# A graph network on one core: a fixed order of issue, an index search on VectorE in place of code matmuls, and a product moved from GpSimd to VectorE

## The chip, the core and the metric

The kernel runs on one core of a Trainium2 chip. A core has five engines that take their instructions in order, each from its own queue: TensorE (PE in the profile, its weight loads PEld), VectorE (DVE), ScalarE (ACT), GpSimd (POOL) and SyncE (SP, which here only issues DMAs). TensorE reads SBUF and writes PSUM[...]. The metric is the device time of one execution in microseconds (us); a profiled execution also gives its span, from its first to its last instruction.

## What is computed

Thirty-two graphs ("batches") of 512 nodes with 128 features and a 512 x 512 adjacency of zeros and ones, with about 3% ones, go through four residual layers. Each starts with `h = max(layernorm(x), 0)`:

```
layer 0: pre = h@(W1-W2) [node i] + h@W2 [node j] + b;  x += max over j of relu(pre) * adj[i,j]
layer 1: four times: tanh([A_rows @ (f@ws+bs), f@wn+bn, A_cols @ (f@wd+bd)] @ wu + bu), with skips
layer 2: x += (adj @ (h@weight)) / rowsum + bias
layer 3: four GRU steps: m = adj^T @ (h@w);  r, z = sigmoid(...);  n = tanh(xn + r*hn)
         h = (1-z)*n + z*h
```

The change touches how layer 0 finds the neighbours of a node, the last line of layer 3, and the order in which everything is issued.

## The kernel before

**Planning.** The Python code runs twice over the work. `prepare`, `gathers`, `layer1` and `layer23` (in `fast`, L858) note each operation in a `Flow` object (L303) with its inputs, outputs and an estimated cost. `Flow.run` (L569) then emits the instructions: of the operations that could start earliest by the estimates, on any engine, it takes the earliest, and among equals that with the earliest due time. A due time is the batch's place in steps of `PACE` less the length of the chain behind the operation (`close`, L436) less a `LEADS` entry for the stage (L41 to L68). Up to `AHEAD` = 6 parts are noted at a time, so several batches are in flight. All of this happens when the program is built; on the chip each engine has one fixed queue. Almost every instruction carries the line of the one emitting call (L529), so the profile's groups are told apart by tile names. Where the planner expects TensorE to idle for over 1 us it adds dummy matmuls (`spin`, L553).

**Layer 0.** The maximum over neighbours is taken in two ways. Columns are cut into eight half-blocks of 64. The first four neighbours within a half-block are picked by one-hot matmuls: `pc` (L1051) counts, `cc` copies the count, 16 DMAs on SP spread it into `ccd`, VectorE or ScalarE makes the one-hot `oh`, TensorE multiplies it with `qhl` into `pa`, and VectorE folds `pa` into `acc`. Neighbours beyond the fourth (up to seven for each node) are fetched as rows from a table in DRAM. For each of four column tiles `it`, TensorE writes keys into `pkey` (L1091, L1092): a matmul with `ltk` gives 1024 times the rank of a neighbour within its half-block, and a matmul with the diagonal `code` adds the row number in the table. VectorE's `max` takes the eight largest keys, and three small operations (`row`, `bad`, `idx`) decode them. The table `qtab` has 1024 rows in an interleaved order (`CODES`), written by four DMAs for each batch (L1041); the rows over 256 are filled with zeros at the start. GpSimd issues 28 indirect DMAs for each batch (`gm`, `G`, L1123), and VectorE folds the results into `gm`.

**Layers 1 to 3.** Wide products use a value split in two (`hi` made by ScalarE, `lo` by VectorE or GpSimd) times the adjacency (`pg`); weight products run on float32 data, which the trace shows as two matmul records each (`pu`, `pk`, `phn`, `pxn`). In a GRU step GpSimd makes `zc = 1-z` (L1305) and `z*h` (L1331, the group `gate<-h,gate`), and VectorE makes the rest; `h` is transposed (`ph`) and split for the next step.

**Setup.** Weights are prepared by `FastWeights` (`first`, `rest`, `last`), with the DMAs dealt in turn to SP and ACT. Batch 0's adjacency, 1 MB, is one DMA on ACT's queue.

Of the kernel before, what the change touches and what calls it, by code (L numbers as in the profile page):

```python
# [17 lines left out]
I32 = mybir.dt.int32  # L18
AF = mybir.ActivationFunctionType
# [11 lines left out]
ROWS = 1024  # L31
KEY = float(ROWS)
CODES = ((0, 1), (P, 1), (2 * P, 2), (4 * P, 4))
ONACT = (2, 2, 1, 0)
NLEFT = 7
PACE = 46.14
SPACING = 1.5
AHEAD = 6
BANKS = (1, 2, 2, 1)

LEADS = {  # L41
    "prepare": -28.3, "counts": -7.5, "keys": 16.5, "rows": 26.6,
    "gather0": 59.4, "gather1": 70.0, "gather2": 28.0, "gather3": 53.5,
    "first": 61.2, "layer1": 43.0, "layer10": 30.3, "layer11": 8.7,
    "layer12": 56.0, "layer13": -41.3, "layer2": 39.7, "layer3": 5.5,
    "layer30": 99.5, "layer31": 189.8, "layer32": 213.5, "layer33": 84.7,
    "out": 56.0,
}

LEADS0 = {  # L50
    "prepare": 18.5, "counts": 53.1, "keys": 4.8, "rows": -15.7,
    "gather0": 52.2, "gather1": 93.4, "gather2": -34.5, "gather3": -69.1,
    "first": 0.5, "layer1": 141.7, "layer10": 10.1, "layer11": 110.3,
    "layer12": -73.8, "layer13": -13.4, "layer2": 6.9, "layer3": 56.5,
    "layer30": 35.3, "layer31": 29.8, "layer32": 117.9, "layer33": 64.0,
    "out": 75.9,
}
LEADSN = {
    "prepare": -19.9, "counts": -18.3, "keys": -42.0, "rows": 46.6,
    "gather0": 15.9, "gather1": -47.7, "gather2": -77.8, "gather3": -4.3,  # L60
    "first": 13.3, "layer1": -33.7, "layer10": 14.0, "layer11": -36.5,
    "layer12": 103.7, "layer13": 62.6, "layer2": 212.2, "layer3": 99.8,
    "layer30": 182.6, "layer31": 105.8, "layer32": 85.0, "layer33": 161.6,
    "out": -15.2,
}
FIRST = (1.57, 0.36, -0.05, 0.0)
LAST = (0.0, 0.18, 0.33, 0.24, 0.3)
WEIGHTS = (-3.98, -2.44, -5.94)  # L68
# [194 lines left out]
class Op:  # L263
    def __init__(self, engine, fn, args, kw, cost, after):
        self.engine, self.fn, self.args, self.kw = engine, fn, args, kw
        self.cost, self.after = cost, after
        self.before, self.next, self.new, self.bufs = [], [], [], []
        self.waits, self.ready, self.due, self.end = 0, 0.0, 0.0, 0.0
        self.issued, self.lane, self.port, self.turn = False, None, False, 0

        self.source = engine if after < 1.0 else id(self)
# [31 lines left out]
class Flow:  # L303
# [11 lines left out]
    EVENT = 0.13  # L315
    ENGINES = ("pe", "vec", "act", "pool", "sync")

    def __init__(self, nc, pace, ahead, slack=0.0):
        self.nc, self.pace, self.ahead, self.slack = nc, pace, ahead, slack
        self.rings, self.part, self.lanes = {}, [], {}  # L320
        self.lead = 0.0
        self.free = dict.fromkeys(self.ENGINES, 0.0)
        self.busy = dict.fromkeys(self.ENGINES, 0.0)
        self.spin, self.window, self.active, self.rate = None, 0, 0.0, 1.0
        self.gathered, self.port, self.turn, self.queue = 0.0, 0.0, 0, {}
        self.seen = {e: {} for e in self.ENGINES}
        self.waiting = {e: [] for e in self.ENGINES}
        self.vec = Engine(self, "vec", nc.vector)
        self.act = Engine(self, "act", nc.scalar)
        self.pool = Engine(self, "pool", nc.gpsimd)  # L330
        self.sync = Engine(self, "sync", nc.sync)
# [22 lines left out]
    def cost(self, engine, op, outs, ins):  # L354
# [9 lines left out]
        if engine == "vec":  # L364
# [4 lines left out]
            else:  # L369
                t = (o if op != "max" else n) / 960.0 + 0.15  # L370
# [11 lines left out]
    def note(self, engine, fn, args, kw, outs, ins, cost, after):  # L382
        op = Op(engine, fn, args, kw, cost, after)
        op.lead = self.lead
# [21 lines left out]

    def spaced(self, lane, gap):

        self.part[-1].lane = (lane, gap)
# [26 lines left out]
    def close(self, n):  # L436

        part, self.part = self.part, []
        inside = {id(op) for op in part}
        lanes = {}  # L440
        for op in part:
            for u in op.before:
                u.next.append(op)
        for op in reversed(part):
            tail = max((u.due for u in op.next if id(u) in inside), default=0.0)
            op.due = tail + op.cost + op.after + self.LAT
            if op.lane:
                lane, gap = op.lane
                op.due = lanes[lane] = max(op.due, lanes.get(lane, 0.0) + gap)
        for op in part:  # L450
            op.due = n * self.pace - op.due - op.lead
            op.waits = sum(not u.issued for u in op.before)
            if not op.waits:
                self.enter(op)
        return part

    def enter(self, op):
        op.ready = max((u.end + u.after + self.lat(u, op) for u in op.before), default=0.0)
        self.waiting[op.engine].append(op)
# [6 lines left out]
    def start(self, op):  # L466
        t = max(op.ready, self.free[op.engine])
        if op.lane:
            t = max(t, self.lanes.get(op.lane[0], -op.lane[1]) + op.lane[1])
# [7 lines left out]
        if op.port:  # L477
            t = max(t, self.port)
        return t

    def step(self):
        best = None
        for e in self.ENGINES:
            now = [(t, op) for op in self.waiting[e] if (t := self.start(op)) is not None]
            if not now:
                continue
            first = min(t for t, _ in now)
            if best is None or first < best[0]:
                t, op = min(
                    ((t, op) for t, op in now if t <= first + self.slack), key=lambda c: c[1].due  # L490
                )
                best = (first, t, op)
        assert best, "nothing can be issued"
        _, t, op = best
        self.waiting[op.engine].remove(op)
# [16 lines left out]
        if op.port:  # L512
            self.port = op.end
        self.busy[op.engine] += cost
        if op.lane:
            self.lanes[op.lane[0]] = t
# [17 lines left out]
        for u in op.next:  # L534
            u.waits -= 1
            if not u.waits:
                self.enter(u)
        self.log(op, t)
# [30 lines left out]
    def run(self, parts):  # L569

        left = []
        of = {}
        oldest = 0
        while True:
            while len(left) < len(parts) and len(left) < oldest + self.ahead:
                n = len(left)
                place, make = parts[n]
                make()
                ops = self.close(place)
                left.append(len(ops))  # L580
                of.update((id(op), (op, n)) for op in ops)
            if oldest == len(parts):
                return
            op = self.step()
            _, n = of.pop(id(op))
            left[n] -= 1
            while oldest < len(left) and left[oldest] == 0:
                oldest += 1
# [34 lines left out]
class FastWeights:  # L623
# [5 lines left out]
    def __init__(self, nc, F, a, const, mid, ps):  # L629
# [28 lines left out]
        self.ltk = fixed([P, P], BF16, "ltk")  # L658
        nc.vector.tensor_scalar(self.ltk, self.lt.bitcast(F32), KEY, None, ALU.mult)
        self.code = fixed([P, n // P, P], BF16, "code")  # L660
        icode, code = fixed([P, n // P], I32, "icode"), fixed([P, n // P], F32, "fcode")
        for t, (first, step) in enumerate(CODES):
            nc.gpsimd.iota(
                icode[:, t : t + 1], pattern=[[1, 1]], base=first, channel_multiplier=step
            )
        nc.vector.tensor_copy(code, icode)
        for t in range(n // P):
            nc.vector.tensor_scalar(
                self.code[:, t, :], ident, code[:, t : t + 1], None, ALU.mult
# [57 lines left out]
    def rest(self):  # L727

        F, a, ident, NL3 = self.F, self.a, self.ident, self.NL3

# [11 lines left out]
        for key, src, m in rows:  # L742
            col[key] = at
            (F.sync, F.act)[len(col) % 2].dma_start(out=brow[at : at + m, :], in_=src)
# [22 lines left out]
        for i in range(NL1):  # L767
# [4 lines left out]
            for k, nm in enumerate(("ws", "wn", "wd")):  # L772
                w = self.temp(("f", "hg", "hT1")[k], f"{nm}{i}")[:, 0:ch, :]
                (F.sync, F.act)[k % 2].dma_start(
# [32 lines left out]
    def last(self):  # L807
# [16 lines left out]
        for l in range(NL3):  # L824
            for nm, dst in (("hh", self.gh), ("ih", self.gm)):
                q = nm == "ih"
                g = self.temp(("gate1", "xn1")[q], f"graw_{nm}{l}")[:, 0:3, :]
                (F.sync, F.act)[q].dma_start(
# [30 lines left out]
def fast(ctx: ExitStack, tc: tile.TileContext, a: dict, out: bass.AP, bad):  # L859
# [11 lines left out]
    F = Flow(nc, PACE, AHEAD)  # L871
    F.share(ps, 8, {f"ps{s}": n for s, n in enumerate(BANKS)} | {"idle": 0})

    def lead(b, stage):
        own = LEADS0 if b == 0 else LEADSN if b == B - 1 else {}
        return LEADS[stage] + own[stage] if stage in own else LEADS[stage]
# [13 lines left out]
    zero = const.tile([P, P], F32, name="zero")  # L890
    nc.gpsimd.memset(zero, 0.0)
    tables, scals = [], []
    for i in range(2):
        t = dram.tile([ROWS, P], F32, name=f"qtab{i}")
        k = (ROWS - 2 * P) // P
        nc.sync.dma_start(
            out=t[2 * P :, :].rearrange("(k p) d -> p k d", p=P),
            in_=zero.unsqueeze(1).to_broadcast([P, k, P]),
        )
        tables.append(F.fixed(t, [ROWS, P], F32))  # L900
# [3 lines left out]
    def load(b):  # L904
# [3 lines left out]
        F.act.dma_start(out=af, in_=adj[b].rearrange("(t p) j -> p t j", p=P))  # L908
# [71 lines left out]
    def prepare(b, xt, af):  # L980
# [60 lines left out]
        for t, (first, step) in enumerate(CODES):  # L1041
            F.sync.dma_start(
                out=tab[first : first + (P - 1) * step + 1 : step, :], in_=qn[:, t, :]
            )
        F.lead = lead(b, "counts")
# [796 lines left out]
```

## Time and profile before

| What | us |
|---|---|
| median of 3 runs (2909.56 to 2911.77) | 2909.67 |
| span of the profiled execution | 2909.0 |
| TensorE busy | 2795.8 |
| VectorE busy | 2299.1 |
| GpSimd busy | 1848.5 |
| ScalarE busy | 1268.4 |

The profiled span lies 0.67 us under the median of the runs, so the two can be read as one number. A stretch of the profile is read by the windows view, which gives each engine's busy time in it. Matmul records overlap their neighbours, since a matmul starts before the one ahead of it has drained; how close TensorE is to packed is therefore read from the distances between starts, not from busy time.

### The profile page before, as it was taken

What the parts mean: (1) busy time and instruction counts of PE and PEld (TensorE: products, weight loads), DVE (VectorE), ACT (ScalarE), POOL (GpSimd) and SP (SyncE); (2) the same over time, 40 slices, a digit from 0 to 9 for tenths busy, and PEclk for the clock granted to TensorE, in tenths of its full rate; (3) what the DMA queues carried; (4) which work ended last, traced back from release to release, by engine and by line L of the source; (5) the groups of instructions that cost most, each with busy time, mean ns of one, the idle gap of its engine ahead of it and who ended that gap; (6) DMA issues with size and microseconds to landing.
All of it is one profiled execution on the core that took longest, in us unless ns stands there. A gap on an engine that the chain in (4) does not pass through costs nothing.

```text
span 2909.0 us, 38588 instructions
## 1 busy us (share of the span) xinstructions
PE 2795.8 (96%) x11766; PEld 1794.6 (62%) x11766; DVE 2299.1 (79%) x5371; ACT 1268.4 (44%) x2622; POOL 1848.5 (64%) x2020
## 2 busy tenths in 40 slices
PE   7799999999999999999999999999999999999998
PEld 4565566666666665666665666666666666566675
DVE  6778888788888888888788888888888888887634
ACT  6643344444444443444443444444444444443333
POOL 3666656666666766666766666776666666666522
PEclk9999999999999999999999999999999999999999
DMA  6644334323444433334423344433344433333200
GB/s 150 136 74 88 62 85 81 83 55 76 79 86 81 83 60 78 74 83 80 87 56 78 74 84 87 82 69 64 74 84 87 81 81 56 70 66 63 55 5 9
DMA packets 191270, 218.49 MB, mean 75 GB/s; under 512 B 30376, under 2 KB 139600, under 8 KB 191056
## 3 DMA queue, kind: packets, MB, share of 16 engines
q0 software_dynamic: 47104, 92.34, 23.1%
q1 hardware_dynamic: 73768, 63.63, 7.1%
q10 hardware_dynamic: 70184, 59.98, 6.8%
q8 instruction: 96, 1.57, 0.2%
q14 instruction: 118, 0.97, 0.1%
HBM read 164.32 MB, written 17.96 MB: 63 GB/s over the span
## 4 chain that ended last, share of the span: by engine, by line
PE 85%; DVE 7%; DMA 2%; issue 2%; ACT 2%; POOL 1%; SPq 0%; ACTq 0%; DVEq 0%; POOLq 0%
PE pg L529 26%; PE pu L529 19%; PE pk L529 14%; PE pa L529 7%; PE phn L529 4%; PE pxn L529 4%; DVE acc L529 3%; PE ph L529 2%; PE pq L529 2%; PE pkey L529 2%; PE pt L529 1%; DVE lo L529 1%; PE pf L529 1%; PE po L529 1%; PE px L529 1%
## 5 line engine op out<-in xcount | busy, mean ns | idle before, releaser
L529 POOL DMA_INDIRECT G<-qtab,idx x768 | 841.3, 1095 | 653.6 <-DVE gm L529 495.3
L529 DVE TENSOR_TENSOR acc<-acc,pa 128x512 f32<-128x512 f32 x992 | 673.4, 679 | 123.3 <-PE pa L529 97.6
L529 PE MATMUL pg<-an,lo 128*128 128x512 f32 (+1 forms) x1072 | 461.9, 433 | 0.0
L529 PE MATMUL pg<-an,hi 128*128 128x512 f32 (+1 forms) x1072 | 456.1, 428 | 4.8 <-PE spin L553 1.1
L529 PE MATMUL pa<-oh,qhl 128*128 128x512 f32 x1024 | 450.5, 508 | 6.1 <-DVE acc L529 2.1
L529 PE MATMUL pu<-ag,w 128*128 128x512 f32 (+1 forms) x952 | 448.0, 568 | 4.1 <-DVE ag L529 4.1
L529 DVE TENSOR_SCALAR oh<-ccd 128x1024 fp32r<-128x1024 bf16 x492 | 348.9, 723 | 62.4 <-PE pa L529 55.0
L529 ACT ACTIVATE xn<-x,shift,rstd 128x128 f32<-128x128 f32 x512 | 214.6, 483 | 261.4 <-POOL shift L529 255.7
L529 PE MATMUL pg<-at,lo 128*128 128x512 f32 (+1 forms) x672 | 295.9, 442 | 22.8 <-DVE lo L529 22.3
L529 PE MATMUL pg<-at,hi 128*128 128x512 f32 (+1 forms) x672 | 272.7, 407 | 8.4 <-ACT hi L529 7.2
L529 PEld LDWEIGHTS pa<-oh,qhl 128*128 128x128 f32 x1024 | 191.8, 193 | 135.5 <-issue 65.9
L529 PEld LDWEIGHTS pg<-an,hi 128*128 128x128 f32 x1072 | 202.6, 189 | 107.2 <-issue 62.5
L529 PEld LDWEIGHTS pg<-an,lo 128*128 128x128 f32 x1072 | 202.7, 189 | 85.9 <-issue 52.0
L529 PE MATMUL pk<-h,g_hh 128*128 128x512 f32 (+1 forms) x528 | 246.7, 582 | 1.2 <-DVE ag L529 1.1
L529 DVE TENSOR_TENSOR gm<-gm,G 128x128 f32<-128x128 f32 x768 | 242.4, 322 | 3.5 <-DMA G<-qtab,idx 3.3
L529 PE MATMUL pk<-mT,g_ih 128*128 128x512 f32 (+1 forms) x528 | 243.3, 580 | 0.5 <-ACT mT L529 0.5
L529 PEld LDWEIGHTS pu<-ag,w 128*128 128x128 f32 x952 | 177.0, 189 | 107.7 <-issue 80.3
L529 ACT ACTIVATE gate<-pk,bsum 128x512 f32<-128x512 f32 (+1 forms) x264 | 176.7, 672 | 151.3 <-PE pk L529 148.7
L529 DVE TENSOR_TENSOR ag<-pg,rbc 128x512 f32<-128x512 f32 (+1 forms) x272 | 172.5, 653 | 71.5 <-PE pg L529 69.7
L529 DVE SCALAR_TENSOR_TENSOR nn<-phn,bcol,gate 128x512 f32<-128x512 f32 (+1 forms) x132 | 96.3, 729 | 148.2 <-ACT gate L529 148.1
L529 ACT COPY mT<-pg 128x512 f32<-128x512 f32 (+1 forms) x164 | 94.3, 575 | 272.9 <-PE pg L529 265.4
L529 POOL TENSOR_TENSOR rstd<-rstd,mhalf 128x4 f32<-128x4 f32 x128 | 152.7, 1193 | 86.9 <-DVE shift L529 82.6
(178 smaller groups left out, 5146.7 us busy)
## 6 DMA issues: line engine op xcount, KB each, us to landing
af<-in_adj_dram ACTq DMA_DIRECT2D x32, 1024.0 KB
ccd<-cc SPq DMA_DIRECT2D x512, 64.0 KB
an<-in_adj_dram POOLq DMA_DIRECT2D x128, 256.0 KB, 3.4
x<-in_x_dram ACTq DMA_DIRECT2D x64, 256.0 KB
rbc<-scal SPq DMA_DIRECT2D x32, 512.0 KB
G<-qtab,idx POOLq DMA_INDIRECT x768, 3.9
qtab<-qn SPq DMA_DIRECT2D x128, 64.0 KB
out_dram<-xo ACTq DMA_DIRECT2D x32, 256.0 KB
```

Source lines behind the costliest of these rows:

```text
L529: op.fn(*(real(v) for v in op.args), **{k: real(v) for k, v in op.kw.items()})
```

## The change

Five things change. (1) The order is no longer found while emitting: every operation has a due time written in a table, a string of three characters for each operation. There are rows for the 3 weight parts, the first 8 batches and the last 10; the 14 batches between share one row, `MIDDLE`, shifted by `PERIOD` = 81.7354 for each. Each engine's queue is its operations sorted by due time; the estimates of costs only decide which queue's head is emitted next and where dummy matmuls go. The due times are keys for sorting. (2) `z*h` is made by VectorE. (3) The keys no longer hold a row number: `ltk` now has a slice for each tile, with 8 + g/8 on the diagonal for half-block g, so the eight largest differ; VectorE's `max_index` finds their columns in the same PSUM tile, and two small operations send absent neighbours to row 512. The 16 `code` matmuls of a batch go. (4) The table has 513 rows in natural order, written by one DMA for each batch, with one zero row set at the start. (5) All weight DMAs are on SP, and batch 0's adjacency is in two halves, on ACT and on SP.

```diff
+MIDDLE = (450.09, ("!!!!WQ!+m!0U...",),)
+FRONT = (...)   BACK = (...)
...
-    def close(self, n):
-            op.due = n * self.pace - op.due - op.lead
+    def queue_up(self, ops):
+        for op in ops:
+            op.waits = len(op.before)
+            for u in op.before:
+                u.next.append(op)
+        self.heads = {e: [] for e in self.ENGINES}
+        for op in sorted(ops, key=lambda op: op.due)[::-1]:
+            self.heads[op.engine].append(op)
...
     def step(self):
-            now = [(t, op) for op in self.waiting[e] if (t := self.start(op)) is not None]
...
+        ops, at = self.starts()
+        e = min(at, key=lambda e: at[e])
+        op, t = ops[e], at[e]
+        self.heads[e].pop()
...
+    def run(self, parts, times):
+        ops = []
+        for make, due in zip(parts, times, strict=True):
+            make()
+            part, self.part = self.part, []
+            for op, t in zip(part, due):
+                op.due = t
+            ops += part
+        self.queue_up(ops)
+        for _ in ops:
+            self.step()
...
-        self.ltk = fixed([P, P], BF16, "ltk")
-        nc.vector.tensor_scalar(self.ltk, self.lt.bitcast(F32), KEY, None, ALU.mult)
+        self.ltk = fixed([P, n // P, P], BF16, "ltk")
+            nc.gpsimd.memset(own[u * HP : (u + 1) * HP, t : t + 1], KBASE + g * HP / n)
+            nc.vector.scalar_tensor_tensor(
+                self.ltk[:, t, :], ident, own[:, t : t + 1], ltf, ALU.mult, ALU.add
+            )
...
-                (F.sync, F.act)[k % 2].dma_start(
+                F.sync.dma_start(
...
-        F.act.dma_start(out=af, in_=adj[b].rearrange("(t p) j -> p t j", p=P))
+        if b == 0:
+            F.act.dma_start(out=af[:, 0:2, :], in_=src[:, 0:2, :])
+            F.sync.dma_start(out=af[:, 2:NT, :], in_=src[:, 2:NT, :])
+        else:
+            F.act.dma_start(out=af, in_=src)
...
-        for t, (first, step) in enumerate(CODES):
-            F.sync.dma_start(
-                out=tab[first : first + (P - 1) * step + 1 : step, :], in_=qn[:, t, :]
-            )
+        F.sync.dma_start(out=tab[0:N, :].rearrange("(t p) d -> p t d", p=P), in_=qn)
...
-                F.mm(pk[:, jt, :], rows, W.ltk, start=True, stop=False, group=pk)
-                F.mm(pk[:, jt, :], rows, W.code[:, jt, :], start=False, stop=True, group=pk)
+                F.mm(pk[:, jt, :], rows, W.ltk[:, jt, :], start=True, stop=True, group=pk)
             F.vec.max(out=top[:, it, :], in_=flat(pk))
-        F.vec.tensor_scalar(row, top, -KEY * (NBASE + KSLOT), ROWS - 1.0, ALU.add, ALU.max)
+            F.vec.max_index(out=at8[:, it, :], in_max=top[:, it, :], in_values=flat(pk))
+        F.vec.tensor_scalar(
+            none, top, KBASE + KSLOT + 1 - HP / (2.0 * N), float(N), ALU.is_lt, ALU.mult
+        )
-        F.vec.tensor_scalar(idx, row[:, :, 0:NLEFT], ROWS - 1, None, ALU.bitwise_and)
+        F.vec.scalar_tensor_tensor(
+            idx, at8[:, :, 0:NLEFT], float(N), none[:, :, 0:NLEFT], ALU.min, ALU.max
+        )
...
-                F.pool.tensor_mul(cut(z, c), cut(h, c), cut(z, c))
+                F.vec.tensor_mul(cut(z, c), cut(h, c), cut(z, c))
...
```

## The prediction

> **What bounds the kernel now.** I read the stretches first (busy time by window), then the chain of waits, then TensorE's timeline in one stretch, then its waits. One stretch of the steady part:
>
> ```profile
> 1036.80:1123.20 86.40, 84.76 (x352) 54.00 (x351) 71.44 (x167) 37.68 (x78) 58.07 (x63) 1.00 0.39 78
> ```
>
> Columns: length, then busy time and instructions of TensorE, its weight loads, VectorE, ScalarE and GpSimd, then the granted clock. TensorE leaves 1.6 us, VectorE 15.0 us. That the stretch is one batch is seen in the chain of waits, where the same piece comes back every 86.4 us:
>
> ```profile
> 1040.80 4.29 PE pu L529 x10
> ...
> 1127.20 4.29 PE pu L529 x10
> ...
> 1215.43 4.29 PE pu L529 x10
> 1301.83 4.29 PE pu L529 x10
> ```
>
> From 432 to 2505.6 us there are 24.0 such periods, so what one of them gains counts 24 times. Is TensorE packed in it? Busy time can't say, so I took distances between starts from the timeline:
>
> ```profile
> 1057.42 0.40 PE L529 MATMUL pg<-an,hi 128*128 128x512 f32 x1
> 1057.65 0.39 PE L529 MATMUL pg<-at,lo 128*128 128x512 f32 x1
> ...
> 1087.74 0.22 PE L529 MATMUL pkey<-code,at 128*128 128x128 bf16 x1
> 1087.79 0.22 PE L529 MATMUL pkey<-ltk,at 128*128 128x128 bf16 x1
> 1087.85 0.22 PE L529 MATMUL pkey<-code,at 128*128 128x128 bf16 x1
> ```
>
> A split product over 512 columns takes 0.228 us; a key matmul 0.056, though its record says 0.22; a record of a float32 product 0.429 (4.29 for ten, above); a float32 transpose or 128-column record 0.108. Counts of one batch from the code: 144 products over 512 columns (104 `pg`, 32 `pa`, 4 `pc`, 4 bias) = 32.8; 90 float32 records (42 `pu`, 48 in the GRU) = 38.6; 57 of 128 columns = 6.2; 8 `pq` of half the columns of a float32 record, 0.215 each = 1.7; 48 bf16 ones (16 `pat`, 32 `pkey`) = 2.7. Sum 82.0 of 86.4: TensorE is the bound, with 4.4 us of gaps in each batch, dummy matmuls among them. Who ends the gaps (TensorE's waits over the whole run):
>
> ```profile
> PE pg L529 <- DVE lo L529: 22.3, 25, 1.1
> PE spin L553 <- DVE lo L529: 9.4, 25, 0.7
> ```
>
> Both come 25 times, once per steady batch: after a transpose, ScalarE makes `hi`, VectorE `lo`, and nothing independent has been put on TensorE's queue meanwhile. That is an order that leaves a hole, not a lack of work.
>
> **What the Trainium skill says.** "Perfetto Trace Analysis", section Identifying the Most-Contended Engine, says matmul busy share is a poor measure; the trace agrees (0.22 us records at 0.056 us distance). "Vector Engine (DVE) Microarchitecture Reference", section 3.9 on the match/index hardware, says that the positions of the eight largest need a load of the values and then a separate pass over the data; no run here shows this yet. "SBUF — State Buffer", section SBUF: two separate sides, says that VectorE with two SBUF inputs and a GpSimd instruction exclude each other on a shared port; the trace agrees in kind: `nn<-nn,zc` takes 0.657 us at least and 1.181 at most in this stretch.
>
> **The change, part by part.**
>
> *Code matmuls.* 16 x 0.056 = 0.9 us of TensorE in each batch, on the bound. Packed work falls to 81.1.
>
> *Index search.* The nearest row and the one like the new product:
>
> ```profile
> L529 DVE TENSOR_TENSOR nn<-nn,zc 128x512 f32<-128x512 f32 x4 | 3.2, 801 | 0.0
> ...
> L529 DVE MAX8 top<-pkey 128x8 f32<-128x512 f32 x4 | 2.6, 682 | 0.8 <-PE pkey L529 0.8
> ```
>
> A search reads the same 512 columns as MAX8: 0.68 us, and I add 0.15 for the load, the length of the shortest operations in this trace (`rstd` 0.155). Four give 3.3 us. From below it is 4 x 0.6 = 2.4 (nothing for the load, overlapped starts); from above 5.5 (two full passes). I take 3.3, because eight values are few. Three small operations remain three (0.17 us each), so decoding is even. The search holds the one kept `pkey` bank (ring `ps0`) another 0.8 us four times; behind it on TensorE wait the next keys and `psc`. This is covered as long as other matmuls stand ahead of them; uncovered it costs up to 3.3 us a batch.
>
> *z\*h.* GpSimd loses 4 x 1.38 = 5.5 us (58.1 to 52.6), VectorE gains 4 x 0.68 = 2.7. The product needs only `h` and the sigmoid, so it can run while ScalarE makes tanh: off the path. But VectorE's queue is in order: if the sigmoid is late, the `acc` maxima that free `pa` banks and the next `oh` stand behind it, and TensorE's `pa` waits for those. Fewer GpSimd instructions also take the shared port less often; I count that as nothing, at most 1 us a batch.
>
> *VectorE in all.* 71.4 + 3.3 + 2.7 = 77.4 us (76.5 to 79.6). With a period of 83 this is 93% busy and 5.6 us idle instead of 15.0. It stays under TensorE's 81.1, but its queue gets tight, and it is the engine that ends TensorE's gaps today.
>
> *Order.* The hole of 3.3 us in the timeline (around 1074 and 1118 us, before `pg`) and small ones make 4.4. A complete order fixed beforehand for a repeated batch can put other batches' matmuls there; it can't remove the time by which VectorE is late against its plan. Between nothing closed (4.4 left) and all closed (0), I take 1.8 left, because VectorE has less slack. The period becomes 81.1 + 1.8 = 82.9: 3.5 less. Over 24 periods 84 us. The table's `PERIOD` is a distance of sorting keys; I take no time from it.
>
> *Table.* SP has four issues of some 0.4 us each for the rows of a batch, then one: 1.2 us less of SP; its queue has little else but `ccd`. TensorE doesn't wait for it. The start writes one zero row instead of two transfers of 384 KB (on the chain at 10.66 us for 4.00 us).
>
> *Start and end.* Batch 0's adjacency is issued at 1.32 us, and its first user starts at 18.99 (`junk`). In two halves on two queues and with 768 KB of zeros gone it comes earlier; but all 17 weight DMAs that ACT issued now stand on SP, 0.25 to 0.45 us each, some 5 us, where the critical `ccd` transfers of the first batches (4.63 and 4.36 us on the chain near 33 and 38 us) are queued too. Net I take 2 us gained (bounds: 8 gained, 6 lost). By the same sum, TensorE's packed work in the first 432 us is 309.5, so 122 us is idle there, mostly filling; a better fill is worth 6 here (0 to 20). The eight batches' worth of work outside the steady part also lose code matmuls, 7 us, of which 4 on the bound. The end is one batch's serial GRU, which no part shortens: 0. Together 12 us.
>
> Sum: 84 + 12 = 96. Span 2909.0 - 96 = 2813; the median lies 0.7 above the span, so 2814 us.
>
> **Rivals.**
>
> *Only the work goes (15%).* The gaps stay 4.4 us or come back in other places because each engine is still in order and `lo` still waits for ScalarE and VectorE. Then 0.9 x 32 = 29 us goes: 2881. For it: `lo` waits on VectorE, which gets busier. Against it: a gap that returns 25 times in one place is closed by moving one group of matmuls.
>
> *VectorE becomes the bound and the kernel slower (12%).* Mechanism: VectorE's present waits (15.0 us a batch, for `pa`, `pg`, sigmoid) don't shrink and the 6.0 us of new work comes on top in its queue: 77.4 + 15.0 = 92.4 a batch, 6.0 more; over 24 periods 144, and 5 more at the ramp, where VectorE is busy 331 of 432 us, 30: 3083 us. The kernel is slower from the point where the waits shrink by less than 6.0 of 15.0 us. For it: `acc` appears in the chain at 3% of the span and at 8% before 432 us. Against it: most of these waits are for TensorE, which is ahead of its work sooner when the period is shorter.
>
> *The order doesn't do on the chip what it says (3%).* One queue's plan is off by a transfer that lands later than foreseen; gains and stalls cancel: 2909.
>
> **How the numbers follow.** My forecast (70%): between 0.5 and 3.4 us of gaps left, a period of 81.6 to 84.5, so 46 to 115 us gained over the steady part, and 4 to 24 outside: 2770 to 2860, likeliest 2814. Only the work goes: 15%; slower: 12%; cancelled: 3%. The range leaves out the slow case, the cancelled one and some of both other cases' edges: 2775 to 2885. What differs by less than 0.2% (6 us) can't be told from no change here. So faster 0.85, same 0.03, slower 0.12.
>
> **What would show it.** Right: the chain's `pu` piece returns after 82 to 84 us; TensorE's waits for `lo` fall below 0.5 us a batch; VectorE is busy for 76 to 80 us of a period; two records per tile for the search, one short and one near 0.68. Wrong: a period over 85, `pg`, `pa` or `phn` waiting for VectorE in every batch, a search over 1.4 us, or a first output, now stored at 280 us, that comes over 10 us later.

## The result, and the profile after

| Kernel | median us | ratio to before [95%] |
|---|---|---|
| before | 2909.6 | |
| after | 2862.7 | 0.984 [0.983, 0.985] |
| forecast | 2814 | 0.967 |

The change gains 47 us where 96 were forecast. The sign was right and the time lies inside the range, but half of the gain is missing. The profiled span is 2864.3 us.

One stretch of the steady part, by the windows view, in the columns of the prediction (length; TensorE, its weight loads, VectorE, ScalarE, GpSimd; clock):

```profile
876.20:960.40 84.20, 83.90 (x334) 51.64 (x333) 78.08 (x179) 37.70 (x78) 55.08 (x58) 1.00 0.43 79
```

VectorE has 6.6 us more than before and 6.1 us left. That this stretch is one batch is again seen in the chain of waits, where one piece returns every 84.1 to 84.6 us (once, near 1123, it is not on the chain):

```profile
954.12 1.77 PE pu L1048 x4
1038.21 1.77 PE pu L1048 x4
...
1207.45 1.77 PE pu L1048 x4
1291.60 1.77 PE pu L1048 x4
```

So the period fell from 86.4 to 84.2 us, not to 82.9. TensorE's waits over the whole run show that the hole named in the prediction is gone (total, times, longest):

```profile
PE ph L1048 <- DVE h L1048: 8.9, 12, 1.3
PE pt L1048 <- ACT xn L1048: 7.8, 9, 3.0
PE pf L1048 <- ACT f L1048: 7.1, 24, 1.2
...
PE pg L1048 <- DVE lo L1048: 0.4, 1, 0.4
```

`pg` and the dummy matmuls together waited 31.7 us for `lo`; now `pg` waits 0.4 for it. No wait for VectorE comes back in every batch. The new operations, in the groups by line:

```profile
L1048 DVE TENSOR_TENSOR gate<-h,gate 128x512 f32<-128x512 f32 (+1 forms) x132 | 90.6, 686 | 21.4 <-POOL zc L1048 12.6 <-issue 8.7
...
L1048 DVE FIND_INDEX8 at<-top,pkey 128x8 uint32<-128x512 f32 x128 | 87.8, 686 | 0.0
L1048 DVE MAX8 top<-pkey 128x8 f32<-128x512 f32 x128 | 87.6, 687 | 9.8 <-PE pkey L1048 8.7 <-PE pt L1048 0.5 <-issue 0.4
...
L1048 DVE MATCH_VALUE_LOAD at<-top,pkey 128x8 f32 x128 | 10.4, 81 | 0.9
```

A search is two records, 0.081 and 0.686 us: 3.1 us a batch.

**Where the 45 us of span come from.** I gave every TensorE record its packed duration (the distances in the prediction; dummy matmuls count as nothing), summed them, and called the rest of the span idle:

| | change in us | prediction |
|---|---|---|
| packed work of TensorE | -28.7 | -29 (0.9 a batch), of which its sum counts 26 |
| idle before 432 us | -10 | -8 (start 2, fill 6) |
| idle from there to 300 us before the end | -24 | -62 (2.6 in each of 24) |
| idle in the last 300 us (30 to 48) | +18 | 0 |

The prediction is wrong in two rows: the steady part, with what follows it, and the end. Within a period I split the idle time by its length. Stalls over 0.13 us (a wait) fell from 3.0 to 1.1 us, dummy matmuls from 0.6 to 0. But stalls below 0.13 us rose from 0.5 us (8 of them) to 1.6 us (24). The timeline shows what they are (start, length, engine):

```profile
875.38 0.39 PE L1048 MATMUL pg<-at,lo 128*128 128x512 f32 x1
875.39 0.19 PEld L1048 LDWEIGHTS pg<-at,hi 128*128 128x128 f32 x1
875.61 0.40 PE L1048 MATMUL pg<-at,hi 128*128 128x512 f32 x1
875.84 0.10 PEld L1048 LDWEIGHTS <-ab 128*128 128x128 bf16 x1 [0.27 <-issue]
875.85 0.23 PE L1048 MATMUL pat<-identb,ab 128*128 128x128 bf16 x1
875.85 0.20 PEld L1048 LDWEIGHTS pg<-an,hi 128*128 128x128 f32 x1
875.88 0.48 PE L1048 MATMUL pg<-an,hi 128*128 128x512 f32 x1
876.20 0.10 PEld L1048 LDWEIGHTS <-ab 128*128 128x128 bf16 x1 [0.15 <-issue]
876.21 0.23 PE L1048 MATMUL pat<-identb,ab 128*128 128x128 bf16 x1
```

One short bf16 transpose and one long product take 0.36 us here (875.85 to 876.21), not 0.056 + 0.228 = 0.284. A long product's weights take 0.19 us to load. Ahead of the product at 875.61 that load began with the previous long product, at 875.39, and was over in time. Ahead of the one at 875.88 it began with the short one, at 875.85, which covers only 0.056 us of it; the record of the product is 0.48 long instead of 0.40. That the uncovered load is what costs the time is my reading of these lines: no run changes the load alone, and 0.13 us uncovered is more than the 0.08 by which the pair is longer. Over the steady part, the median cost of a bf16 matmul that stands alone is 0.136 us by the starts around it, in a run 0.056 each. Before, 48 of them stood in 5 runs per batch (4, 8 or 24 long). The fixed order fits them in one by one: 32 in 23 runs, 19 of these of length one.

### The profile page after: what moved, and what is told of

It reads as the page before. It is cut to its first block, busy times and chain, and to the rows that moved or that the text cites. A ratio compares the mean times of both kernels' runs of the same rounds, so it can differ in the third digit from the quotient of the medians.

```text
span 2864.3 us, 37049 instructions
## 1 busy us (share of the span) xinstructions
PE 2784.9 (97%) x11230; PEld 1727.7 (60%) x11230; DVE 2491.5 (87%) x5757; ACT 1272.7 (44%) x2622; POOL 1738.8 (61%) x1892
## 3 DMA queue, kind: packets, MB, share of 16 engines
q0 software_dynamic: 47104, 92.34, 24.4%
## 4 chain that ended last, share of the span: by engine, by line
PE 58%; DVE 19%; issue 9%; ACT 5%; POOL 4%; DMA 2%; SPq 1%; DVEq 0%; ACTq 0%; POOLq 0%
PE pg L1048 19%; PE pk L1048 11%; PE pu L1048 9%; DVE acc L1048 6%; PE pa L1048 5%; PE phn L1048 3%; DVE oh L1048 3%; PE pxn L1048 3%; DVE nn L1048 2%; POOL rstd L1048 2%; POOL G L1048 2%; DVE lo L1048 2%; PE ph L1048 1%; PE pf L1048 1%; ACT xn L1048 1%
## 5 line engine op out<-in xcount | busy, mean ns | idle before, releaser
L1048 POOL DMA_INDIRECT G<-qtab,idx x768 | 829.7, 1080 | 522.0 <-DVE gm L1048 259.3
L1048 PE MATMUL pa<-oh,qhl 128*128 128x512 f32 x1024 | 535.3, 548 | 6.1 <-DVE acc L1048 2.1
L1048 PE MATMUL pg<-an,hi 128*128 128x512 f32 (+1 forms) x1072 | 446.5, 418 | 0.4 <-DVE lo L1048 0.4
L1048 PE MATMUL pg<-an,lo 128*128 128x512 f32 (+1 forms) x1072 | 428.0, 405 | 0.3
L1048 DVE TENSOR_SCALAR oh<-ccd 128x1024 fp32r<-128x1024 bf16 x492 | 374.5, 771 | 2.8 <-PE pa L1048 1.5
L1048 PE MATMUL pg<-at,hi 128*128 128x512 f32 (+1 forms) x672 | 291.5, 441 | 2.3 <-ACT oh L1048 1.4
L1048 PE MATMUL pg<-at,lo 128*128 128x512 f32 (+1 forms) x672 | 278.9, 418 | 1.0 <-POOL lo L1048 0.8
L1048 POOL TENSOR_TENSOR rstd<-rstd,mhalf 128x4 f32<-128x4 f32 x128 | 190.4, 1488 | 109.5 <-DVE rstd L1048 92.1
L1048 PE MATMUL pk<-mT,g_ih 128*128 128x512 f32 (+1 forms) x528 | 252.8, 583 | 0.4 <-ACT mT L1048 0.3
L1048 POOL DMA_INDIRECT gm<-qtab,idx x128 | 133.3, 1041 | 99.7 <-issue 86.2
```

Of the source, the lines that this page charges most:

```text
L1048: op.fn(*(real(v) for v in op.args), **{k: real(v) for k, v in op.kw.items()})
```

## Experiments

Theory S: the missing part of the steady gain is spent on short matmuls that stand alone. Rival V: it is spent on VectorE's full queue, the mechanism of my slower case. Who brought the 47 us, the order or the operations, was a second question.

**e2: the search taken out.** It leaves the neighbour numbers out: instead of searching, a small operation converts the eight keys, so that other rows are fetched.

```diff
-            F.vec.max_index(out=at8[:, it, :], in_max=top[:, it, :], in_values=flat(pk))
+            F.vec.tensor_scalar(at8[:, it, :], top[:, it, :], 1.0, None, ALU.mult)
```

> The changed kernel without the pass over the keys: the eight numbers are made from the eight keys by a small operation, so the rows fetched are not the neighbours' rows; everything else stays. VectorE has about 3.0 us less a batch. Theory V (VectorE's full queue stretches the period): the period falls from 84.2 by 1 to 3 us, time 2790 to 2835. Theory S (TensorE loses the time where short matmuls stand alone between long ones): the period falls by less than 0.4 us, time 2850 to 2865.

Measured: 2863.6 us, 0.984 [0.982, 0.986], the same as after. The windows view of the same stretch:

```profile
876.20:960.40 84.20, 83.60 (x331) 51.35 (x330) 76.31 (x175) 37.65 (x78) 54.76 (x59) 1.00 0.43 79
```

VectorE has 1.8 us less to do and the period is unchanged: V falls as the reason for 84.2. (The small operation takes back part of the 3.1 us, so a larger relief isn't tested here.)

**e4: short matmuls grouped.** From the sixth batch on, the four keys of a column tile, and the four bf16 transposes of a half tile, get one due time, the latest of the four (or that of a following group, where it is earlier), and so stand together.

```diff
             ops += part
+            last = {}
+            for op in part if 2 * len(part) > 1207 and part[0].due > 150 else ():
+                name = op.args[0].tile.args[2] if op.engine == "pe" else ""
+                if name.startswith(('pkey', 'pat')):
+                    last.setdefault((name, name[:3] == "pat" and op.args[0].steps[0][1][1]), []).append(op)
+            t = 1e9
+            for same in list(last.values())[::-1]:
+                t = min(t, max(op.due for op in same))
+                for op in same:
+                    op.due = t
```

> The changed kernel, but from the sixth batch on the four key matmuls of a tile, and the four bf16 transposes of a tile's half, stand together on TensorE's queue, at the place of the last of them. A lone bf16 matmul takes 0.136 us of TensorE in the trace, one in a group 0.056. Theory S: some 13 fewer places a batch x 0.08 us = 1.0 us less, period 83.2, time 2830 to 2845. Theory V: no change or a little slower, 2855 to 2875, since the first of a group comes later.

Measured: 2838.5 us, 0.975 [0.974, 0.977]. The windows view and TensorE's timeline:

```profile
869.00:952.20 83.20, 82.73 (x333) 52.51 (x332) 78.20 (x179) 37.61 (x78) 55.05 (x58) 1.00 0.43 80
```

```profile
871.23 0.39 PE L1048 MATMUL pg<-at,lo 128*128 128x512 f32 x1
871.46 0.62 PE L1048 MATMUL pat<-identb,ab 128*128 128x128 bf16 x8
871.89 0.47 PE L1048 MATMUL pg<-an,hi 128*128 128x512 f32 x1
```

Eight transposes from 871.46 to 871.89 cost 0.43 us; eight alone would cost 8 x 0.136 = 1.09. Runs per batch fall from 23 to 6, stalls under 0.13 us from 1.6 to 0.55 us, longer ones rise a little (1.1 to 1.3). The period is 83.2, 1.0 less; 24 periods give 24 us, which is the whole difference to after (and by the same ledger the middle row loses another 24.7 us of idle time, the last row nothing). VectorE is as busy as in after (78.20 and 78.08 us), so V doesn't explain the gain. S is shown as far as the price goes: the bf16 matmuls that stand alone cost 1.0 us a period. This version beats both kernels.

**e7: float32 transposes grouped as well**, where that leaves the order of the PSUM tiles as it is.

```diff
+        new = [op.due for op in ops if op.engine == "pe" and op.new]
+        for group in groups:
+            group.sort(key=lambda op: op.due)
+            t = group[-1].due
+            clear = not any(group[0].due < d <= t for d in new)
+            for op in group if clear else group[1:]:
+                op.due = t
```

> The grouped kernel (2838.5) with one more edit: float32 transposes that fill one PSUM tile stand together on TensorE's queue too, where that leaves the order of the PSUM tiles as it is. In the planned order of one batch the float32 transposes that stand alone fall from 12 to 5. Theory S (a short matmul that stands alone costs 0.08 to 0.09 us more than one in a run): 7 times 0.09 is 0.6 us a period, 15 us over the steady part: 2820 to 2828. Theory W (what is left is waits on other engines, and the later first transposes make new ones): 2835 to 2860.

Measured: 2848.3 us, 0.978 [0.977, 0.980], 10 us slower than e4. Single ones fell from 10 to 4 a batch, but the period became 83.4 and the first output was stored at 289 us instead of 283. Stalls didn't shrink (short ones 0.64, long ones 1.4 us). Either S doesn't carry over to them, or grouping at the latest due time has a price of its own that hides the gain; I didn't separate the two.

**e9, e10: the new operations in the old order.** The planner of before is left to plan the old operations, 20,352 in all, and the new ones are issued in the places of the old: each search right behind its max (`both`), nothing for a code matmul. e10 has the last line of this edit alone. What is left to the kernel after is the order itself, the first transfers and the table's one write (e9 keeps four for each batch).

```diff
-                F.mm(pk[:, jt, :], rows, W.ltk, start=True, stop=False, group=pk)
-                F.mm(pk[:, jt, :], rows, W.code[:, jt, :], start=False, stop=True, group=pk)
+                F.mm(pk[:, jt, :], rows, W.ltk[:, jt, :], start=True, stop=True, group=pk)
+                F.mm(pk[:, jt, :], rows, W.ltk[:, jt, :], start=True, stop=True, group=pk)
+                F.part[-1].fn = nothing
...
+            both(F.part[-1], at8[:, it, :], top[:, it, :], flat(pk))
...
                 F.pool.tensor_mul(cut(z, c), cut(h, c), cut(z, c))
+                F.part[-1].fn = F.nc.vector.tensor_mul
```

> The kernel before with its order kept op for op (20,352 planned operations in the same sequence), and the new operations put in it: z*h on VectorE, the search right behind each max, no code matmuls; first transfers as before. What then is left to the kernel after is the fixed order and the first transfers. Theory O (the gain is the order's; the operations bring at most the code matmuls' 29 us): 2880 to 2920. Theory Z (z*h on VectorE relieves GpSimd and the port in any order, 80 us in the new one): 2800 to 2870. Theory V (6.0 us more in VectorE's queue make it late where TensorE waits for lo): 2930 to 3080, as under the old planner (3076).

> The kernel before with its order kept op for op; only z*h is issued to VectorE instead of GpSimd, at the place it had in the sequence. Theory Z: 2820 to 2880. Theory O: within 10 us of 2910. Theory V: slower, 2925 to 2990. The planner's own version of this edit took 3035, in an order that it changed.

Measured: e9 2942.4 us, 1.012 [1.010, 1.014]; e10 2900.4 us, 0.998 [0.997, 0.998]. In the old order z\*h gains 8 us, and the search with the code matmuls gone loses 42. TensorE's waits of e9 say how:

```profile
PE pg L528 <- DVE at L905: 30.2, 49, 1.0
PE spin L552 <- DVE lo L528: 16.1, 25, 0.7
PE pg L528 <- DVE lo L528: 13.6, 25, 0.8
```

L905 is the search: 49 times, about twice in each steady batch, `pg` starts when a search ends, though it doesn't read what the search finds. It may take over the PSUM tile whose keys the search still reads; that isn't shown. An output is stored every 88.0 us. This is my slower rival at work, at a fifth of its size (34 us where it said 173), in the order that wasn't made for these operations. The same operations in the fixed order take 2863: the order, with the first transfers and the one table write, is worth 80 us, and the operations alone, put in the old places, lose 34.

**e3: z\*h back on GpSimd, in the fixed order.**

```diff
-                F.vec.tensor_mul(cut(z, c), cut(h, c), cut(z, c))
+                F.pool.tensor_mul(cut(z, c), cut(h, c), cut(z, c))
```

> The changed kernel with z*h back on GpSimd, same order. VectorE has 2.7 us less a batch, GpSimd 5.5 us more. Theory V: 2800 to 2845. Theory S: 2850 to 2870, and slower still if GpSimd's longer product makes the GRU step late.

Measured: 2942.3 us, 1.012 [1.010, 1.013]. I had counted the relief of GpSimd as nothing; here it is 80 us. VectorE's timeline, then GpSimd's, around two GRU steps:

```profile
888.43 2.10 DVE L1048 TENSOR_TENSOR nn<-nn,zc 128x512 f32<-128x512 f32 x1 [0.66 <-ACT nn L1048]
...
961.54 1.55 DVE L1048 TENSOR_TENSOR nn<-nn,zc 128x512 f32<-128x512 f32 x1 [0.22 <-ACT nn L1048]
```

```profile
887.58 1.08 POOL L1048 DMA_INDIRECT G<-qtab,idx  x1 [0.16 <-DVE nn L1048]
888.69 1.28 POOL L1048 TENSOR_TENSOR gate<-h,gate 128x512 f32<-128x512 f32 x1
...
961.25 1.29 POOL L1048 TENSOR_TENSOR gate<-h,gate 128x512 f32<-128x512 f32 x1
```

GpSimd's products end at 889.97 and 962.54, and each `nn` ends 0.55 us later, long after its own 0.69. The groups by line of e3, then of after, and VectorE's and TensorE's waits of e3:

```profile
L1048 DVE TENSOR_TENSOR nn<-nn,zc 128x512 f32<-128x512 f32 (+1 forms) x132 | 155.5, 1178 | 64.8 <-ACT nn L1048 59.8 <-POOL zc L1048 3.9 <-POOL rstd L1048 0.8
L1048 DVE TENSOR_TENSOR nn<-nn,zc 128x512 f32<-128x512 f32 (+1 forms) x132 | 88.6, 672 | 6.1 <-ACT nn L1048 3.6
...
DVE h L1048 <- POOL gate L1048: 52.8, 32, 3.4
...
PE ph L1048 <- DVE h L1048: 24.4, 45, 2.3
PE pa L1048 <- DVE oh L1048: 15.6, 22, 0.8
```

Over the run `nn<-nn,zc` takes 1.178 us in the mean, against 0.672 in after: 132 x 0.506 = 67 us, in the middle of the serial GRU step, and TensorE's `ph` waits for `h` 45 times (24.4 us) instead of 12 (8.9). "SBUF — State Buffer", section SBUF: two separate sides, says that a VectorE instruction with two SBUF inputs and one of GpSimd that reads SBUF share a port under an exclusive lock: what starts first has it for its whole length. The second pair agrees. In the first, `nn` begins 0.26 us before the product and waits all the same; an indirect DMA's issue on GpSimd ran until 888.66, and whether that held the port isn't shown.

That the port brings all of the 80 us isn't shown. There is a rival in the same trace: `h` waits 32 times, 52.8 us in all, for GpSimd's product, which is then the last of its inputs to come. In after VectorE makes the product itself and that wait is gone. e3 doesn't separate the two.

**e1, e5, e6, e11: the old planner makes the order itself.** e1 has all new operations, e5 only z\*h on VectorE, e6 only the search with the new first transfers. e11 takes e5's order and issues z\*h to GpSimd, so that all operations are those of before. The first added line is e5's, both are e11's:

```diff
-                F.pool.tensor_mul(cut(z, c), cut(h, c), cut(z, c))
+                F.vec.tensor_mul(cut(z, c), cut(h, c), cut(z, c))
+                F.part[-1].fn = F.nc.gpsimd.tensor_mul
```

> All operations of the changed kernel (index search, z*h on VectorE, one table write, first transfers), but ordered by the planner of the kernel before. Theory A (the fixed order is worth something beyond the removed matmuls): slower than the changed kernel by 15 to 40 us, 2878 to 2900. Theory B (only the removed code matmuls count, 29 us): like the changed kernel, 2860 to 2880. If VectorE's added work hurts under an order that was not made for it, it comes out at 2900 or above.

> The kernel before with one edit: z*h on VectorE instead of GpSimd, the planner and all other operations as they were. In the new order the same move was worth 80 us (2942 with z*h on GpSimd, 2863 with it on VectorE). Theory P (GpSimd's load and its exclusion with VectorE are dear in any order): 2830 to 2900. Theory Q (what the move is worth depends on the order; under the old one VectorE's queue gets late): 2920 to 3080, and together with the run that adds the search alone about the 166 us that both add under the old planner.

> The kernel before with the index search in place of the code matmuls and the new first transfers, z*h left on GpSimd, the old planner. In the new order leaving the search out gained nothing. If the search is free in any order: 2880 to 2915 (code matmuls' 29 us gained at most). If VectorE's queue under the old order is what made both together slower: 2950 to 3080, at least a third of the 166 us.

> The converse: the planner is told that z*h is VectorE's and makes the order that took 3035, but z*h is issued to GpSimd, so that every operation is that of the kernel before. If the planner's order is what costs (any other input to it loses the one regular pattern that it fell into): 3000 to 3060. If the operation costs: 2900 to 2930.

Measured: e1 3076.4 (1.057 [1.056, 1.059]), e5 3034.8 (1.042 [1.041, 1.044]), e6 3050.3 (1.048 [1.046, 1.050]), e11 3101.6 us (1.067 [1.065, 1.069]). After e1 I read its 166 us as the price of the operations. e11 has none of them and is slower still by 25: the planner's order costs this, not the operations. In the steady part before stores an output every 86 to 88 us, mostly every 86.4; e5 every 77 to 107, e6 every 77 to 109. Theory Q in e5's expectation (VectorE's queue late) isn't needed for that, and the sum of e5's and e6's loss, 264, is not 166. In this irregular order too z\*h on VectorE gains 67 us (e11 to e5). So before's 86.4 hung on one regular pattern, which its planner lost with each of the three changed inputs.

**e8: the old first transfers**, except for the table's single zero row.

```diff
-                F.sync.dma_start(
+                (F.sync, F.act)[k % 2].dma_start(
...
-            F.sync.dma_start(out=af[:, 2:NT, :], in_=src[:, 2:NT, :])
+            F.act.dma_start(out=af[:, 2:NT, :], in_=src[:, 2:NT, :])
```

> The kernel after with its first transfers as before: the weights' DMAs issued alternately by SP and ACT, and the second half of batch 0's adjacency on ACT as well; the one zero row of the table is kept. If the new first transfers bring the 2 us that the prediction took, up to 8: 2865 to 2871. If the weights' 17 issues on SP cost what they bring: 2859 to 2865. If they hurt (the first output came 5 us later than before): 2855 to 2859.

Measured: 2867.9 us, 0.985 [0.984, 0.987]: 5 us slower than after, near what two measurements can tell apart.

**Not tried.** No experiment changes the end alone, and none separates the port from a late GpSimd.

## Why the prediction was half right

*Code matmuls, 0.9 us a batch.* Right: packed work fell by 28.7 us over 32 batches.

*Order: gaps from 4.4 to 1.8 us, period 82.9.* The mechanism was right: the hole before `pg` closed, the waits for `lo` went. The step that failed is the 1.8 us of gaps that I left on TensorE: by the same sum it measured 84.2 - 81.1 = 3.1 us, so the period is 84.2 and gains 2.2 us instead of 3.5. Over 24 periods that is 31 us of the 49 that are missing. My reason for leaving any, that VectorE has less slack, isn't what holds the period (e2), and waits alone fell to 1.1 us, below my 1.8. What I left out is that filling a hole by single short matmuls costs TensorE: 1.0 us more a batch than the runs of before. I had priced `pkey` and `pat` from a run of them, at 0.056, and let them be moved anywhere at that price. e4 takes that term away and is at 83.2, with 2.1 left. "TensorE: Matmul & The Clock Gate", section Back-to-back issue gap, says that the spacing of matmuls is set by the weight load and the matmul together. The trace agrees in kind, with 0.136 us for the lone one, but not with the section's figure of about 81 ns for 128 columns: in a run they take 0.056. I priced by the matmul in a run alone.

*VectorE 77.4 us, search 3.3, z\*h 2.7.* Right: 78.1, 3.1 and 2.7. That VectorE stays under the bound is right for the fixed order: e2 gains nothing. In the old order, though, the same operations cost 34 us (e9).

*z\*h's relief of the port counted as nothing.* Wrong for this order: 80 us (e3), against 8 in the old one (e10), where `nn` took 0.832 us in the mean with `z*h` on GpSimd, not 1.178. The fixed order leans on the move: without it the kernel is slower than before (e3). That the relief is the port's is argued: where the move gained much, `h` had waited long for GpSimd's product too (52.8 us in e3, 41.4 in e11, 4.0 in before).

*Start and end, 12 us.* The start gained 10 of idle time against the 8 that I gave (and 5 of it may be the transfers, e8), though the first output came 4 us later. The end was taken as 0 and lost 18; that is the second step that failed. Before, the last two outputs were stored at 2898 and 2899 us, their GRUs side by side; after, at 2802 and 2854, and the last batch is alone. The windows view of the last 84 us, first after, then before:

```profile
2780.00:2864.30 84.30, 64.79 (x314) 43.77 (x312) 32.74 (x93) 27.69 (x60) 10.64 (x17) 0.95 0.03 8
```

```profile
2825.00:2909.00 84.00, 70.52 (x321) 48.81 (x319) 36.58 (x93) 32.70 (x69) 23.95 (x31) 0.95 0.03 8
```

TensorE is busy 5.7 us less there. "No part shortens the GRU" was true; I should have asked what runs beside it. The same sum over the other traces says that it goes with the order: the last 300 us hold 28 to 30 us of idle time in e9 and e10, which keep before's order, and 47 to 53 in e2, e3, e4, e7 and e8, which keep the fixed one or a grouped form of it. That the lone last batch is the reason isn't shown by an experiment.

*Rivals.* "Only the work goes" (2881) is in part right: gaps do come back elsewhere, but 3.1 us of the 4.4, not all. "VectorE becomes the bound" (3083) is not what happened; in before's own order the operations do cost time, but far less, 2942.

## What to carry to other kernels

When an order closes waits on a packed TensorE, price what it fills them with as it will stand there: here a short bf16 matmul between long ones cost more than twice what it costs in a run. To tell an order from operations, keep the order op for op and swap what is issued; letting a greedy planner plan anew measures the planner. And look at the last batch by itself: what leaves the steady part earlier may run alone at the end.

## What was not expected of the hardware

- A lone 128x128 bf16 matmul among float32 products over 512 columns costs 0.136 us of TensorE, one in a run 0.056. The next product's weight load of 0.19 us, which it doesn't cover, is the likely reason, not a shown one. For float32 transposes the distances looked alike (0.20 alone, 0.108 in a run), yet grouping them gained nothing (e7).
- VectorE's position search of eight values over 512 columns takes as long as the search for their maxima: 0.686 and 0.687 us.
- A product of 0.69 us on VectorE took 2.10 beside a GpSimd product of 1.28 us (e3): it waited for 1.4, longer than that product. An indirect DMA's issue of 1.08 us stood ahead of that product on GpSimd.
